# Transposes pinned directly ahead of the way up, statistics later in the tiles, and two reads moved, in a one-core transformer block

## The chip, the cores and the metric

The kernel runs on one core of a Trainium2 chip. A core has five engines, each with its own queue of instructions that it works off in order: PE (TensorE, matmuls and transposes; its weight loads, PEld, overlap with its matmuls), DVE (VectorE), ACT (ScalarE), POOL (GpSimd) and SP (SyncE, which here only issues DMAs). They meet at semaphores. Sixteen DMA engines move data between HBM and the core's memory. The metric is the device time of one execution in microseconds (us), here the median of several runs.

## What is computed

One block of a Perceiver-like transformer on x of 32 x 64 rows of 512 numbers, in fp32, cut to its core:

```python
x = x + xattn(layernorm(x), ctx, mask)          # softmax(x ctx^T / sqrt(512)) ctx, 256 context rows a batch
x = x + mla(layernorm(x), ...)                  # 16 heads, low-rank q (384) and kv (128), wo: 2048 -> 512
x = x + ffn(layernorm(x), ...)

def ffn(h):
    logits = h @ gate_w                                       # 8 experts
    scale = top_k(logits, 2).sum()
    shared = square(relu(h @ up_w)) @ down_w                  # 512 -> 2048 -> 512
    y = shared + (h @ expert_weight) * scale
    return layernorm(y) * ln_gamma + ln_beta
```

## The kernel before

**Stages.** The 2048 rows are 16 tiles of 128 rows (two batches). In the profiled execution the tile loop (lines 512 to 600) runs from 0 to about 240 us: cross attention, first residual, the latent q and kv. Then the attention itself (240 to 550), the way out (wo, L1073 to L1143, 551 to 765), the way up (up_w, from L1145, 773 to about 930) and the way down (down_w, 930 to 1097). PE works on fp32r, so an operand is split into a part h, rounded to fp32r (a copy by ACT, L147), and the rest l (a subtraction by DVE, L149), and a product is three matmuls: h h, h l, l h. The three large products also use a scheme with seven products of half blocks in place of eight; its sums ahead are POOL's, its sums behind are `combine` (one ACT copy L160, then DVE L162, L163, L165, L166, L168). The way out has 8 blocks of 256 rows by 8 values of k, 64 units u; the way up has 4 row blocks b by 8 units k, in the order `ORDER = (0, 1, 5, 6, 7, 2, 3, 4)`, of 42 matmuls each. A unit writes four PSUM banks, of which there are two sets; it can write a bank when the combine of the unit two before has read it.

**Order of work.** A framework's scheduler fixes the order on each engine's queue at compile time, by a model of its own, and sets the semaphores. `after(ins)` and the `pins` arguments say only that what follows is ordered behind `ins` in that order; they are no waits on the chip.

**The tile loop.** Iteration i scores tile i, reads out tile r = i - 1 (residual, normalisation with index b) and makes latents of tile q = i - 2. `stats(i + 1)` is the layer norm's statistics of the tile after the next: two DVE steps lnst_a, lnmv_a (L133, L135), DVE's rst_a (L123) and POOL's power rs_a (L127). For i of 4 to 14 it is written ahead of `a_q`; for i of 1 to 3 it stands behind `rooted["b.."]`, DVE's rst_b of tile r. `norm` then makes xn (DVE, L139) with rs_a; `a_x` does the same with rs_b. Both go through PE transposes (psy) and the split xh (ACT), xl (DVE L149). `psc` are PE's transposes of the next context.

**The way out.** For unit u, `left(u + 2)` splits the operand hl; `seven` does the matmuls (L723 with the high part first, L725 with the low). Weights for a unit are reads (`read_slot`) and splits (`put_slot`, two ACT casts wh and two DVE subtractions wl) into slots, the weights of wo first, those of the way up (`"up"`) in the last block's units: `UP_READ` and `UP_PUT` are the units of u % 8 of that block. After a block's last unit DVE adds the residual (`ox`, 512 KB, `o_load`, L948), normalises (`on`), PE transposes it (`ops`, L985), ACT and DVE split it (oh, ol), PE multiplies with the gate and the expert (`cpe`, `mm3` at L175), DVE takes the two largest (MAX8, gs), ACT scales (mo) and stores it (`mod<-mo`), and beta is added (`oo<-oo,beb`, L974). Beta is read once, broadcast to all partitions (256 KB), through POOL's queue at L922; the first residual at unit 10.

**The way up.** The split of its left operand is `right` (xr_0 and xr_2 by ACT, xr_1 and xr_3 by DVE). `settle(8, ...)` puts 8 PE transposes of a weight (their result is not used) ahead of the first products; with `None` as pin they are free to be placed by the scheduler:

```python
with after(settle(8, ps, wh[:, 0, 0], ident2, None) if b == 0 else None):
```

After each unit ACT squares the result (L1226, L1227), and in the first five units of b = 0 `put_slot(ORDER[n + 3], "up", pins=pins)` splits the weights of the unit three later.

Of the kernel before, what the change touches and what calls it, by code (L numbers as in the profile page):

```python
# [18 lines left out]
P = 128  # L19
B, S, D = 32, 64, 512  # L20
M = 256
NT = (B * S) // P
# [19 lines left out]
ORDER = (0, 1, 5, 6, 7, 2, 3, 4)  # L42
# [13 lines left out]
MULT_AT = (21, 25, 31, 39, 47, 55, 63)  # L56

FEATURES_AT = (2, 4)
UP_READ, UP_PUT = (1, 2, 5, 6, 7), (3, 5)

BETA_AT = 60

# [24 lines left out]
def perceiver_block(ctx: ExitStack, tc: tile.TileContext, x, mem, mask, wq_a, bq_a, qnw, wq_b, bq_b,  # L87
                    wkv_a, bkv_a, kvnw, wkv_b, wo, bo, gate, up, down, expert, gamma, beta, cs, out):
    nc = tc.nc
# [51 lines left out]
    def after(ins):  # L141
        return tc.issue_after(ins.ins) if ins is not None else ExitStack()
# [32 lines left out]
    def mm3(ps, pairs):  # L175

        n = len(pairs)
        for j, (ah, al, bh, bl) in enumerate(pairs):
            nc.tensor.matmul(ps, ah, bh, start=(j == 0), stop=False)  # L179
            nc.tensor.matmul(ps, al, bh, start=False, stop=False)  # L180
            nc.tensor.matmul(ps, ah, bl, start=False, stop=(j == n - 1))  # L181


    with ExitStack() as mla:
# [25 lines left out]
        with ExitStack() as pa:  # L210
# [145 lines left out]
            def stats(i):  # L356
                return ln_stats(sp, xts[i], 1e-5, f"a{i}")
# [157 lines left out]
            for i in range(NT + 2):  # L515
                q, r = i - 2, i - 1
                do_q, do_r = q >= 0, 0 <= r < NT
                if 1 <= i and i + 1 < NT:
                    if i > 1:
                        load_x(i + 1)  # L520
                    load(i + 1)
                if i == 1:
                    load_vectors()
                if i == 4:
                    load_turns()
                if do_q and i % 2 == 0:
                    hp[q // 2] = load_raw(q // 2)
                if i < NT:
                    with after(scored[0] if i == 1 else None):
                        cT = [a_t(i, 0), a_t(i, 1)]  # L530
                if 3 < i and i + 1 < NT:
                    mr = stats(i + 1)
                if do_q:
                    qk = ap.tile([P, 576], FP, tag="qk", bufs=1, name=f"qk{q}")
                    xh, xl, _ = xx.pop(q)
                    a_q(q, 0, qk, xh, xl)
                if do_r:
                    ex, rv = so.pop(r)
                    eT = a_e(r, ex)
                if i == 1:  # L540
                    prep_wa(1, raws[1])
                if do_q and i != NT:
                    a_q(q, 1, qk, xh, xl)
                    if i != 2:
                        lat = a_p(q, qk)
                if do_r:
                    x1 = a_r(r, eT, rv)
                if i == 2:
                    lat = a_p(q, qk, stats_of[f"b{r}"])
                if 1 <= i <= 3:  # L550
                    with after(rooted[f"b{r}"]):
                        mr = stats(i + 1)
                if i < NT:
                    xT = a_xT(i)
                if i == 1:
                    prep_wa(2, raws[2])
                if i == NT:
                    a_q(q, 1, qk, xh, xl)
                    lat = a_p(q, qk)
                if do_q and i % 2 == 1:  # L560
                    hp[q // 2] = fold_q(q // 2, *hp[q // 2])
                if q >= 2 and i % 2 == 0:
                    fold_o(q // 2 - 1, *hp.pop(q // 2 - 1))
                if do_q and i % 2 == 0:
                    hp[q // 2] += (load_rkv(q // 2),)
                if do_r:
                    xn = a_n(r, *x1)
                if do_q:
                    lat = a_z(q, *lat)
                if i < NT:  # L570
                    so[i] = a_s(i, cT, xT)
                if i == 1:
                    prep_wa(3, raws[3])
                    prep_wa(4, raws[4])
                if do_r:
                    xx[r] = a_x(r, xn)
                if do_q:
                    a_k(q, *lat)
                if i == 0:
                    last = prep_wa(0, raws[0])  # L580
                    load_small(masks[0])
                    with after(last[1]):
                        mr = stats(1)
                if i + 1 < NT:
                    norm(i + 1, mr)
                if i in (NT - 3, NT - 2):
                    load_q(i - NT + 3)
                if i in (NT - 2, NT - 1):
                    for k in range(NKQ):
                        split_q(i - NT + 2, k, xx[r][2])  # L590
# [3 lines left out]
        with ExitStack() as pb:  # L594
# [248 lines left out]
            n = len(units)  # L843
# [75 lines left out]
    sp = pc.enter_context(pool("o_small", 2))  # L919
    psb = ExitStack()  # L920
    beb = ap.tile([P, D], FP, name="beb")
    nc.gpsimd.dma_start(beb, beta.partition_broadcast(P))  # L922
    pss[1] = banks(psb.enter_context(pool("o_psb", space=PSUM)), "op1")
    oc = ExitStack()
    ocp = oc.enter_context(pool("o_c", 2))
# [7 lines left out]
    def o_load(blk):  # L933
        xt = ap.tile([P, 2, D], FP, tag="xt", name=f"ox{blk}")
        nc.sync.dma_start(xt, x1_d[blk].rearrange("t p d -> p t d"))
        return xt
# [65 lines left out]
    def o_expert(blk, xh, xl, _):  # L1002

        mo = mos.pop(blk, None) or ap.tile([P, 2, D], FP, tag="mo", name=f"mo{blk}")
        for tt in range(2):
            i = 2 * blk + tt
            sl = slice(tt * P, (tt + 1) * P)
            pes = []
            for c in (slice(256, NE), slice(0, 256)):
                pe = ps_t.tile([P, D], FP, tag="T", name=f"cpe{i}_{c.start}")  # L1010
                mm3(pe[:, 0 : c.stop - c.start], [
                    (xh[:, k, sl], xl[:, k, sl], wes[0][:, k, c], wes[1][:, k, c]) for k in range(NKD)
                ])
                pes.append(pe)
            t8 = sp.tile([P, 8], FP, tag="t8", name=f"t8{i}")
            nc.vector.max(t8, pes[0][:, 256:264])
            gs = sp.tile([P, 1], FP, tag="gs", name=f"gs{i}")
            nc.vector.tensor_tensor(gs, t8[:, 0:1], t8[:, 1:2], ALU.add)
            if tt:
                yield  # L1020
            nc.scalar.mul(mo[:, tt, 256:512], pes[0][:, 0:256], gs)
            nc.scalar.mul(mo[:, tt, 0:256], pes[1][:, 0:256], gs)
        nc.scalar.dma_start(mo_d[blk], mo)
        yield

    xr, xc, xw = {}, {}, []

    def read_x(b, kk, room=None, behind=None):

# [43 lines left out]
    for u, (blk, k) in enumerate(out_units):  # L1073
# [20 lines left out]
            read_slot(ORDER[i], "wo", i < 6, reads[-1])  # L1094
        if u in SLOT_AT:
            put_slot(ORDER[3 + SLOT_AT.index(u)], "wo", pins=low)
        if u == 10:
            xt[0] = o_load(0)
        if u == 30:
            with after(low[0]):  # L1100
                nc.scalar.copy(ident2, ident)
# [33 lines left out]
    xT = o_t(NB - 1, xns.pop(NB - 1), lambda: next(scaled))  # L1135
    for part in range(3):
        right(0, part, (dones[NB - 1][0], xT[2][1]))
    put_slot(ORDER[2], "up", pins=xT[2])
    for _ in o_expert(NB - 1, *xT):
        pass  # L1140
    pc.close()


# [2 lines left out]
    with ExitStack() as pu:  # L1146
# [3 lines left out]
        def up_seven(ps, k, b, n, steps):  # L1150
            wh, wl = (t[:, 0:7].rearrange("p a (k f) -> p a k f", k=2) for t in wts[k])

            def product(s, parts, first=False, last=False):
                i, j = SEVEN[s]
                for m, (kk, w, low) in enumerate(parts):
                    nc.tensor.matmul(  # L1156
                        ps[s // 2][:, s % 2], w[:, i, kk], xr[b, 2 * kk + low][:, j],
                        start=(first and m == 0), stop=(last and m == len(parts) - 1),
                    )

            most = [(0, wh, 0), (0, wl, 0), (0, wh, 1), (1, wh, 0), (1, wl, 0)]
            rest = [(1, wh, 1)]
            one, two = (0, 2, 4, 6), (1, 3, 5)
            late = None
            if n == 0:
                with after(settle(8, ps, wh[:, 0, 0], ident2, None) if b == 0 else None):
                    for s in one:
                        product(s, most, first=True)
            if n == 7:
                for s in one:  # L1170
                    product(s, rest, first=True)
                for s in (0, 2, 4):
                    product(s, most, last=True)
                for s in two:
                    product(s, rest, first=True)
                if b + 1 < NB // 2:
                    late = right(b + 1, 3)
            for s in range(7):
                if n == 0 and s in one:
                    product(s, rest, last=True)  # L1180
                elif n < 7:
                    product(s, most + rest, True, True)
                elif s in two or s == 6:
                    product(s, most, last=True)
                if s in (1, 3, 5, 6):
                    with after(late if s == 3 else None):
                        next(steps)
# [238 lines left out]
```

## Time and profile before

| | us |
|---|---|
| median of three runs | 1103.54 (1102.34 to 1108.92) |
| the profiled execution | 1098.9 |
| its span, first to last instruction | 1096.7 |
| PE busy | 1066.9 |
| DVE busy | 769.0 |
| ACT busy | 546.1 |
| POOL busy | 508.1 |

The clock granted to PE was full (1.00) in every stretch looked at. In the profile a line of a timeline gives start, busy time, engine, line and operation, output<-input, shape, and in square brackets the engine's idle time just before it and what ended that. A pair of tiles in the loop takes 27.4 us in steady state; a unit of the way up takes 4.95 us. A wait list counts only the waits of one engine, by who ended them.

### The profile page before, as it was taken

Reading aid. Unit: us, or ns where it says so; the run is one execution under the profiler, and the core shown is the slowest. Engines: PE = TensorE matmul, PEld = TensorE weight load, DVE = VectorE, ACT = ScalarE, POOL = GpSimd, SP = SyncE. Lnnn points to the kernel's source line nnn. Section 1 sums busy time; section 2 is a strip of 40 time slices with the busy share of each in tenths; the row PEclk is TensorE's granted clock in tenths of the full one; section 3 lists DMA queues with packets and bytes.
Section 4 is the critical chain, followed back from the end, with each engine's and each line's share of the span. In section 5 each row is a group of like instructions: output and inputs, shape, how many; then the busy total and the mean of one; then the engine's idle time right before and its main releaser. Section 6 shows DMA issues by size and latency. Waiting matters only on the chain.

```text
span 1096.7 us, 26072 instructions
## 1 busy us (share of the span) xinstructions
PE 1066.9 (97%) x10201; PEld 983.6 (90%) x10201; DVE 769.0 (70%) x1369; ACT 546.1 (50%) x1051; POOL 508.1 (46%) x691
## 2 busy tenths in 40 slices
PE   8999999999999999999998999999999999999996
PEld 6667777679999999999988999999999999999996
DVE  5666666657666666656787866667785658898786
ACT  4444444533433444434475544445676567755553
POOL 2333333326788778874570000003238970065671
PEclk9999999999999999999999999999999999999999
DMA  8867666343776778655487776779646689998672
GB/s 259 263 216 231 206 212 203 124 161 121 260 234 245 260 247 294 249 207 195 160 324 276 263 241 213 231 235 359 218 156 202 221 247 366 310 309 257 206 232 79
DMA packets 195386, 254.67 MB, mean 232 GB/s; under 512 B 18544, under 2 KB 140032, under 8 KB 195264
## 3 DMA queue, kind: packets, MB, share of 16 engines
q1 hardware_dynamic: 190704, 240.92, 67.0%
q10 hardware_dynamic: 3456, 8.39, 2.2%
q0 software_dynamic: 1104, 3.70, 0.9%
q8 instruction: 80, 1.31, 0.5%
q14 instruction: 42, 0.34, 0.1%
HBM read 146.67 MB, written 106.30 MB: 231 GB/s over the span
## 4 chain that ended last, share of the span: by engine, by line
PE 59%; DMA 10%; POOL 9%; DVE 8%; issue 7%; ACT 5%; SPq 1%; DVEq 0%; POOLq 0%; ACTq 0%
PE up L1156 9%; PE pss L773 5%; PE psq L179 4%; PE psq L180 4%; PE psq L181 4%; PE op L725 3%; PE op L726 3%; PE op L723 3%; PE psv L817 3%; DMA hd<-uo 2%; PE pse L179 2%; PE pse L181 2%; PE pse L180 2%; DMA x1d<-xt 2%; DMA vd<-vw 2%
## 5 line engine op out<-in xcount | busy, mean ns | idle before, releaser
L755 DVE SCALAR_TENSOR_TENSOR qe<-pse,bqp,cq 64x256 f32<-64x256 f32 x256 | 123.7, 483 | 76.5 <-PE pse L181 70.7
L1156 PE MATMUL up<-xr,wh_up 128*128 128x256 f32 x896 | 157.6, 280 | 0.6 <-DVE uo L168 0.6
L1156 PEld LDWEIGHTS up<-xr,wh_up 128*128 128x128 f32 x896 | 137.5, 189 | 1.0 <-issue 0.7
L725 PE MATMUL op<-wh_wo,hl 128*128 128x256 f32 x448 | 124.4, 279 | 3.7 <-DVE hl L149 3.7
L723 PE MATMUL op<-wh_wo,hl 128*128 128x256 f32 x448 | 124.0, 280 | 0.6 <-ACT hl L147 0.6
L725 PE MATMUL dp<-wh_down,hl 128*128 128x256 f32 x448 | 124.5, 278 | 0.0
L723 PE MATMUL dp<-wh_down,hl 128*128 128x256 f32 x448 | 124.4, 278 | 0.0
L726 PE MATMUL dp<-wl_down,hl 128*128 128x256 f32 x448 | 124.3, 277 | 0.0
L149 DVE TENSOR_TENSOR hl<-c,hl 128x896 fp32r<-128x896 f32 x84 | 94.3, 1126 | 42.3 <-ACT hl L147 42.0
L1156 PE MATMUL up<-xr,wl_up 128*128 128x256 f32 x448 | 123.7, 280 | 0.0
L726 PE MATMUL op<-wl_wo,hl 128*128 128x256 f32 x448 | 123.5, 277 | 0.0
L147 ACT CAST hl<-c 128x896 fp32r<-128x896 f32 x84 | 79.0, 942 | 77.7 <-PE op L726 38.0
L179 PE MATMUL psq<-qa_hi,qh 128*128 128x256 f32 x384 | 112.5, 293 | 0.0
L180 PE MATMUL psq<-qa_hi,ql 128*128 128x256 f32 x384 | 106.4, 277 | 0.0
L181 PE MATMUL psq<-qa_lo,qh 128*128 128x256 f32 x384 | 106.2, 276 | 0.0
L725 PEld LDWEIGHTS op<-wh_wo,hl 128*128 128x128 f32 x448 | 84.3, 188 | 4.8 <-DVE hl L149 4.7
L723 PEld LDWEIGHTS op<-wh_wo,hl 128*128 128x128 f32 x448 | 83.6, 188 | 1.5 <-ACT hl L147 0.8
L723 PEld LDWEIGHTS dp<-wh_down,hl 128*128 128x128 f32 x448 | 84.6, 189 | 0.0
L725 PEld LDWEIGHTS dp<-wh_down,hl 128*128 128x128 f32 x448 | 84.1, 188 | 0.4 <-DVE hl L149 0.4
L1156 PEld LDWEIGHTS up<-xr,wl_up 128*128 128x128 f32 x448 | 84.2, 188 | 0.0
L726 PEld LDWEIGHTS op<-wl_wo,hl 128*128 128x128 f32 x448 | 84.1, 188 | 0.0
L726 PEld LDWEIGHTS dp<-wl_down,hl 128*128 128x128 f32 x448 | 84.1, 188 | 0.0
(233 smaller groups left out, 3146.6 us busy)
## 6 DMA issues: line engine op xcount, KB each, us to landing
c<-vd SPq DMA_DIRECT2D x58, 448.0 KB, 4.2
cx<-in_ctx SPq DMA_DIRECT2D x32, 512.0 KB, 4.6
vd<-vw SPq DMA_DIRECT2D x29, 512.0 KB, 3.6
hd<-uo SPq DMA_DIRECT2D x107, 128.0 KB, 3.3
hd<-uw SPq DMA_DIRECT2D x21, 512.0 KB, 3.3
dcw<-hd SPq DMA_DIRECT2D x18, 448.0 KB, 5.6
vd<-v SPq DMA_DIRECT2D x30, 256.0 KB, 3.5
wd_wo<-pw_wo SPq DMA_DIRECT2D x8, 896.0 KB, 4.9
```

Source lines behind the costliest of these rows:

```text
L147: copy = nc.scalar.copy(hi, src)
L149: return copy, engine.tensor_tensor(lo, src, hi.bitcast(FP), ALU.subtract)
L179: nc.tensor.matmul(ps, ah, bh, start=(j == 0), stop=False)
L180: nc.tensor.matmul(ps, al, bh, start=False, stop=False)
L181: nc.tensor.matmul(ps, ah, bl, start=False, stop=(j == n - 1))
L723: first = nc.tensor.matmul(ps[s // 2][:, s % 2], h[:, a], wh[:, b], start=(k == 0 and s % 2 == 0), stop=False)
L725: nc.tensor.matmul(ps[s // 2][:, s % 2], l[:, a], wh[:, b], start=False, stop=False)
L726: ins = nc.tensor.matmul(ps[s // 2][:, s % 2], h[:, a], wl[:, b], start=False, stop=last)
L755: rope = nc.vector.scalar_tensor_tensor(qe[64 * a : 64 * a + 64, :], pe[r, :], bqp[r, p : p + 1], cq[r, a, :], ALU.add, ALU.mult,)
L773: nc.tensor.matmul(ps[64 * j : 64 * j + 64, pj, b, :], qs[2 * pj + j][a][:, sl], kT[:, a, kt], start=(a == 0), stop=(a == 1),)
L817: nc.tensor.matmul(o, kv[a, i, :], t[a, bp, :], start=True, stop=True)
L1156: nc.tensor.matmul(ps[s // 2][:, s % 2], w[:, i, kk], xr[b, 2 * kk + low][:, j], start=(first and m == 0), stop=(last and m == len(parts) ...
```

## The change

It has five parts.

1. `mm3` returns its last matmul and `o_expert` keeps it; before the way up there are 4 instead of 8 transposes, pinned behind the last `cpe` matmul.
2. `UP_PUT` loses its second unit; the split of slot `ORDER[1]` of the way up is called after the last `right` of the way out, pinned behind `xT[2]` (the last split of oh and ol).
3. `stats(i + 1)` stands behind rst_b in all iterations.
4. Beta's read goes from POOL's queue to SP's, behind the first residual.
5. The first residual's read goes from unit 10 to unit 12, pinned behind the reads issued so far.

```diff
-UP_READ, UP_PUT = (1, 2, 5, 6, 7), (3, 5)
+UP_READ, UP_PUT = (1, 2, 5, 6, 7), (3,)
...
-            nc.tensor.matmul(ps, ah, bl, start=False, stop=(j == n - 1))
+            ins = nc.tensor.matmul(ps, ah, bl, start=False, stop=(j == n - 1))
+        return ins
...
-                if 3 < i and i + 1 < NT:
-                    mr = stats(i + 1)
...
-                if 1 <= i <= 3:
+                if 1 <= i and i + 1 < NT:
                     with after(rooted[f"b{r}"]):
                         mr = stats(i + 1)
...
     beb = ap.tile([P, D], FP, name="beb")
-    nc.gpsimd.dma_start(beb, beta.partition_broadcast(P))
...
-                mm3(pe[:, 0 : c.stop - c.start], [
+                made.append(mm3(pe[:, 0 : c.stop - c.start], [
...
-        if u == 10:
-            xt[0] = o_load(0)
+        if u == 12:
+            with after(reads[-1]):
+                xt[0] = o_load(0)
+                nc.sync.dma_start(beb, beta.partition_broadcast(P))
...
     for part in range(3):
         right(0, part, (dones[NB - 1][0], xT[2][1]))
+    put_slot(ORDER[1], "up", pins=(low[0], xT[2][1]))
     put_slot(ORDER[2], "up", pins=xT[2])
     for _ in o_expert(NB - 1, *xT):
         pass
+    ends = made[-1]
...
-                with after(settle(8, ps, wh[:, 0, 0], ident2, None) if b == 0 else None):
+                with after(settle(4, ps, wh[:, 0, 0], ident2, ends) if b == 0 else None):
```

In the order of the changed program, ACT's half of slot `ORDER[1]` stays where it was and DVE's half stands behind the copies xr_1, ahead of the next slot's; the four transposes stand between the last `cpe` matmul and the first matmul of the way up; and in the first eight units of the way up ACT and DVE take units 2 and 3, 4 and 5, 6 and 7 in pairs, where they took one after the other.

## The prediction

> **What bounds the kernel now.** I read the page first, from its busy shares to the chain that ended last:
>
> ```profile
> PE 1066.9 (97%) x10201; PEld 983.6 (90%) x10201; DVE 769.0 (70%) x1369; ACT 546.1 (50%) x1051; POOL 508.1 (46%) x691
> PE 59%; DMA 10%; POOL 9%; DVE 8%; issue 7%; ACT 5%; SPq 1%; DVEq 0%; POOLq 0%; ACTq 0%
> ```
>
> TensorE (PE) is busy 1066.9 of 1096.7 us, so an edit off PE counts only where it opens or closes a gap in PE. Second, windows over the stages touched (columns: window; length; busy us of PE, PEld, DVE, ACT, POOL; granted clock; DMA share; GB/s):
>
> ```profile
> 155.00:182.00 27.00, 26.64 (x187) 19.36 (x188) 17.55 (x44) 12.89 (x34) 9.51 (x21) 1.00 0.64 205
> 580.00:600.00 20.00, 16.94 (x140) 16.34 (x140) 14.48 (x18) 11.44 (x15) 0.00 (x0) 1.00 0.75 256
> 773.00:816.00 43.00, 42.43 (x363) 42.25 (x362) 35.53 (x56) 31.41 (x54) 12.11 (x15) 1.00 0.46 147
> ```
>
> The tile loop loses 0.36 us in 27, the way out 3.06 in 20, the way up 0.57 in 43. Third, who ends PE's waits (total, times, longest):
>
> ```profile
> PE op L725 <- DVE hl L149: 3.7, 4, 2.0
> PE psq L292 <- DVE x L434: 3.2, 7, 1.9
> PE ops L985 <- DVE on L139: 1.0, 1, 1.0
> PE cpe L179 <- ACT oh L147: 0.9, 2, 0.5
> PE up L1156 <- DVE uo L168: 0.6, 1, 0.6
> ```
>
> These five are what the change can win: 9.4 us, of which it reaches about 6 (below).
>
> **Part 1, the statistics.** In tiles 4 to 14 the three steps lnst_a, lnmv_a, rst_a (0.69, 0.18, 0.15 us) move behind rst_b. In an even tile the order on DVE is now:
>
> ```profile
> 169.57 0.15 DVE L123 TENSOR_SCALAR rst_b<-lnmv_b 128x1 f32<-128x1 f32 x1
> 170.41 0.55 DVE L139 TENSOR_SCALAR xn<-x,lnmv_b,rs_b 128x512 f32<-128x512 f32 x1 [0.70 <-POOL rs_b L127]
> 170.88 0.54 DVE L139 TENSOR_SCALAR xn<-xt,lnmv_a,rs_a 128x512 f32<-128x512 f32 x1
> 172.33 0.69 DVE L149 TENSOR_TENSOR xl<-psy,xh 128x512 fp32r<-128x512 f32 x1
> ```
>
> Both normalisations run in one breath after one wait for POOL. In the new order, lnst_a fits into that 0.70 wait and costs nothing; without that cover it is 0.69 per tile. But lnmv_a and rst_a now stand behind xn(b), and the second xn waits for POOL's rs_a, which starts only then: 0.18 + 0.15 + 0.57 (POOL's step) + 0.1 of hand-overs, so 170.88 becomes about 171.9. Behind it in DVE's queue stand the score step, the maximum and xl; the PE transposes of the context that start at 173.07, when xl has ended (172.33 + 0.69), start 0.8 to 1.0 later. Tile 2 already has this order, and shows the price:
>
> ```profile
> 33.45 0.73 DVE L139 TENSOR_SCALAR xn<-xt,lnmv_a,rs_a 128x512 f32<-128x512 f32 x1 [0.60 <-POOL rs_a L127]
> 35.17 0.66 PE L373 MATMUL psc<-ident,cx 128*128 128x128 f32 x4 [0.56 <-DVE xl L149]
> ```
>
> Six even tiles (4 to 14) at 0.9 give +5.4; the ends are 0.56 (tile 2) and 1.02 (all of the delay), so 3.4 to 6.1. Odd tiles normalise one tile only; tile 3, which has the new order too, took 12.62 us against 12.73 to 12.83 of later odd tiles: -0.1 on six, -0.6. In tile 5 lnst_a waits 2.02 us for the load xt (landed 67.2) with everything behind it; that is the 1.88 us gap of PE at 71.95, and the tile takes 16.30 us instead of 14.63. Issued later, it finds xt landed: -1.7. Next late there is nothing that the trace shows. Sum +3.1 (+1.1 to +4.4).
>
> **Parts 2 and 3, beta and residual.** Beta (256 KB) leaves POOL's queue (issue 569.66, 0.58 us, which come free for the sums and stores of vd behind it; counted inside the bound below) and stands on SP behind the residual (512 KB), which moves from issue 578.07 to two units later. Around 577 to 586 the DMA engines are full (share 1.02 in 560 to 580, 397 GB/s), and the weight vd of the way out lands 586.6, releases wl_wo at 586.89, that hl at 588.90, that PE at 590.04 after 2.05 us. Some 768 KB fewer in that stretch are at most 768/415 = 1.9 us; I take 1.6 of the gap's 2.05; two smaller gaps before it (0.62 at 584.13, where hl waits for a read landed 583.1, and 0.39 at 585.25) I leave as they are. What is late next: the same 768 KB now stand on SP ahead of a c read; the residual's add (1.22 us) goes ahead of hl of unit 16, whose slack (from its end to PE's first low product) is 0.98, and beta's add (1.21) ahead of hl of unit 19, slack 0.05: up to 0.2 + 1.2. DVE idles 0.84 ahead of one hl there (612.28, for ACT), which swallows part; I put 0.6 back. Sum -1.0; from -2.5 (the gaps of 2.05 and of 0.48 at 615.74 closed) to +1.4 (both adds stall in full, nothing won).
>
> **Parts 4 and 5, the settling transposes and slot ORDER[1].** Taking wl of that slot (2.63 us at 755.37) out from ahead of combine(7) lets the last normalisation start earlier, but its first wait is then PE's cpe (MAX8 at 763.22): -0.83 of the 1.02 and 0.43 gaps (ops waiting for on, cpe for oh). Of the 8 transposes, before, 3 and 4 lie in these gaps (765.75, 767.01) and one on the path (773.04); after, four lie on it, 0.11 each: +0.33. So the way up starts at about 772.6 instead of 773.07. The granted clock in 760 to 775 is 1.00 with 1.45 us of idle, and in 580 to 600 with one gap of 2.05; so I price fewer transposes at nothing more.
>
> The Trainium skill speaks against that: "TensorE: Matmul & The Clock Gate", Part 4 (PE-mode transpose), says transposes do not count as busy for the clock gate, and its table ("Why this matters") has an idle window of about 3 us drop the clock to half. By the page the stretch from 763.65 to 767.4 (gap, transposes, gap) would have been one such window already; the trace shows no drop. By it, one slow window would add an estimated 1.7 us to the sum; I leave it out.
>
> On DVE wl of ORDER[1] (2.0) now stands ahead of wl of ORDER[2], the last MAX8/gs and xr_3. From 770.99 - 0.83: wl to 772.2, wl to 774.2, MAX8/gs to 774.6, xr_3 in two halves to 775.5 and 776.8, while PE wants them at 774.9 and 776.2 or so: +1.2 in unit 0. The last mo leaves ACT after gs: its store is issued about 776.5 instead of 774.17, and the first L162 of the way up, which waits for that buffer, goes from 780.10 to about 782.4.
>
> Worst, the scheduler has turned the queues: where ACT and DVE now take one unit after another,
>
> ```profile
> 785.37 2.09 DVE L149 TENSOR_TENSOR wl_up<-wl_up,wh_up 128x1024 fp32r<-128x1024 f32 x2 [0.89 <-ACT wh_up L147]
> 790.10 2.10 DVE L149 TENSOR_TENSOR wl_up<-wl_up,wh_up 128x1024 fp32r<-128x1024 f32 x2 [0.32 <-ACT wh_up L147]
> ```
>
> with a pitch of 4.73 against PE's 4.95 per unit, the changed program orders units in pairs: both L160, both L162, both combines, acts, wh, acts, wh, then wl twice. That is a loop through two engines per pair: 1.4 (two L162) + 1.6 (rest of one combine) + 1.7 (acts after L168) + 1.7 (wh) + 2.1 (acts) + 1.7 (wh) + 1.4 (the last wl) = 11.6 us, against 9.9 of PE. Three pairs lose 1.7 each, 5.1, of which the slack of the first (about 1.1: wl ends 787.4, PE needs it at 788.0, and the L163 slack) is free, plus the 2.3 of the late store: 6.3, and unit 0's 1.2 is mostly swallowed by the same wait, not added. Carried through rows with these durations, unit 8 starts about 820.4 instead of 813.39 (+7.0); against the same chain for the old order, +7.6. I take +6.5 for parts 4 and 5 together. Ends: 2.5 (the store lands in its old 780.1 and half the pair loss is hidden) and 7.6.
>
> **Sum.** 3.1 - 1.0 + 6.5 = +8.6. The profiled execution took 1098.9 us (span 1096.7 and 2.2 around it); it becomes 1107.5. The median of the runs, 1103.5, lies 4.6 higher; with the same addition, 1112.1: slower by 0.8%, inside the 1% (11 us) that a measurement of this kernel can tell from no change.
>
> **Rivals.**
> *Faster.* The DMA relief decides: tile 5's wait (-1.7), the gap at 590.04 (-2.05) and the transition (-0.83) all close, and POOL's rs_a comes before xn(b) has ended in even tiles, and the pairs stay within PE's slack. For it: the two largest waits in the list are just these. Against: tile 2's 0.56. It decides if even tiles lose under 0.3 (6 x 0.3 = 1.8): -4.6 + 1.8 - 0.6 = -3.4 at most, and so about 1100. 0.15.
> *The pairs are hidden*, since an engine's queue is eager where the data are there: U costs 1, tiles 3.1, way out -1.0: +3.1, 1106.6. Against: 4.73 against 4.95 leaves only 0.2 per unit. 0.20.
> *Everything in full.* Tiles 4.4, way out +1.4, way up 7.6: +13.4, 1117. It decides if the two adds stall hl. 0.20.
> *The change does less than it says*: ACT's half of ORDER[1] stays in its place, only DVE's moves, and seven of eight transposes were free. This is in the sum already; alone it leaves 1103.5.
>
> **Numbers.** Forecast (1109 to 1115) 0.45, rivals 0.15, 0.20, 0.20. Range 1102 to 1119: it leaves out most of the faster case (0.10) and the end of the full one (0.06). Faster by over 1% would need 11 us, more than the five waits hold: 0.04. Slower by over 1% (above 1114.6): the full case and a third of the forecast's, 0.35. Within: 0.61.
>
> **What would show it.** In the changed profile: DVE's xn of even tiles waiting 0.5 to 0.6 for POOL rs_a, and PE's psc for xl six times; no 1.88 at tile 5; PE's up waiting for wl and L163 by 0.5 to 2 us in units 3 to 8; the mo store near 776.5; the op wait at 590 under 1 us. I am wrong if psc shows no wait, or if the eight units stay at 4.95.

## The result and the profile after

The changed kernel takes 1112.65 us (median of 11 runs, 1108.59 to 1116.76), the kernel before 1102.34 us in the same series (11 runs): ratio 1.0084, 95% interval 1.0067 to 1.0102. It is slower: by 9.3 us if the ratio is taken, by 10.3 if the two medians are subtracted. The profiled execution took 1109.2 us, its span 1107.0 against 1096.7.

The page after, busy shares and the chain that ended last:

```profile
PE 1065.6 (96%) x10197; PEld 980.7 (89%) x10197; DVE 767.5 (69%) x1369; ACT 544.6 (49%) x1051; POOL 507.4 (46%) x690
PE 52%; issue 12%; POOL 12%; DVE 9%; DMA 9%; ACT 6%; SPq 1%; DVEq 0%; POOLq 0%; ACTq 0%
```

The engines do the same work; PE's share falls because the span is longer. The windows that answer to those of before (the last begins and ends 5 and 10 us later, with the stage):

```profile
155.00:182.00 27.00, 25.62 (x180) 18.38 (x179) 16.89 (x43) 12.15 (x33) 9.10 (x18) 1.00 0.64 211
580.00:600.00 20.00, 16.72 (x138) 15.94 (x138) 14.61 (x14) 11.47 (x14) 3.51 (x4) 1.00 0.73 262
778.00:826.00 48.00, 43.41 (x362) 42.37 (x361) 37.26 (x61) 29.75 (x52) 11.79 (x12) 1.00 0.42 133
```

The tile loop now idles 1.38 us in 27 (0.36 before), the way out 3.28 in 20 (3.06), the way up 4.59 in 48 (0.57 in 43). And who ends PE's waits:

```profile
PE op L724 <- DVE hl L149: 5.7, 6, 2.0
PE psc L374 <- DVE xl L149: 5.4, 7, 0.8
PE up L1158 <- DVE uo L162: 3.3, 1, 3.3
PE dp L722 <- DVE up L163: 1.9, 1, 1.9
PE psq L293 <- DVE x L435: 1.6, 7, 0.2
PE up L1158 <- DVE xr L1063: 1.3, 2, 0.9
```

psc waiting for xl is the loop's new wait (0.6 before), L162 and xr are the way up's, and the wait of 1.9 us at the entry of the way down is new against this profile of the kernel before (its second profile, below, has it too). The longest wait for hl in the way out is still 2.0.

Where the 10.3 us of the two spans lie, by the starts of PE's matmuls of each stage (first scores; last latent transposes; first and ninth unit of the way up; and so on), in us:

| profile | start | tile loop | attention | way out | units 0-7 | rest of way up | way down | span |
|---|---|---|---|---|---|---|---|---|
| before | 9.74 | 222.95 | 318.74 | 221.64 | 40.31 | 117.78 | 165.51 | 1096.68 |
| changed | 8.95 | 226.89 | 319.86 | 222.28 | 45.24 | 117.70 | 166.05 | 1106.95 |

The loop lost 3.9 and the first eight units of the way up 4.9. The rest, 1.4 us, is spread over stages that the change does not touch, or touches without a clear effect. One profile is one execution: the way out took 221.6 to 229.3 us in five profiles that have it in the same form (the two of the kernel before, e1, e5, e6), so its 0.6 us here says nothing.

### The profile page after: what moved, and what is told of

Its sections match the earlier page's. It is cut to its first block, busy times and chain, and to the rows that moved or that the text cites. A ratio compares the mean times of both kernels' runs of the same rounds, so it can differ in the third digit from the quotient of the medians.

```text
span 1107.0 us, 26074 instructions
## 1 busy us (share of the span) xinstructions
PE 1065.6 (96%) x10197; PEld 980.7 (89%) x10197; DVE 767.5 (69%) x1369; ACT 544.6 (49%) x1051; POOL 507.4 (46%) x690
## 3 DMA queue, kind: packets, MB, share of 16 engines
q8 instruction: 80, 1.31, 0.5%
## 4 chain that ended last, share of the span: by engine, by line
PE 52%; issue 12%; POOL 12%; DVE 9%; DMA 9%; ACT 6%; SPq 1%; DVEq 0%; POOLq 0%; ACTq 0%
PE pss L772 5%; PE up L1158 5%; PE psq L179 4%; PE psq L180 4%; PE psq L181 4%; PE op L724 3%; PE op L725 3%; PE op L722 3%; PE psv L816 3%; POOL uw L155 2%; POOL c L155 2%; PE pse L179 2%; PE pse L181 2%; PE pse L180 2%; POOL dcw L155 2%
## 5 line engine op out<-in xcount | busy, mean ns | idle before, releaser
L1158 PE MATMUL up<-xr,wh_up 128*128 128x256 f32 x896 | 155.0, 278 | 5.2 <-DVE uo L162 3.3
```

The costliest lines, as they stand in the source:

```text
L1158: nc.tensor.matmul(ps[s // 2][:, s % 2], w[:, i, kk], xr[b, 2 * kk + low][:, j], start=(first and m == 0), stop=(last and m == len(parts) ...
```

## The experiments

### Each part alone

Four kernels hold one part each: `stats(i + 1)` moved (e1), slot `ORDER[1]` moved (e2), the two reads moved (e3), 4 pinned transposes (e4). The edits are the lines of the diff above that belong to the part.

> The kernel before with the statistics alone moved. Theory: the loop loses what it lost in the changed kernel, whose tiles took 12.62 and 15.71 us in turn instead of 12.73 and 14.63: PE waits for xl in six even tiles (about 1.1 us each), tile 5's wait of 1.9 us is gone; +3.9 us at the end of the loop and at the end of the kernel, ratio about 1.0035. Rival: a later stage has waits that swallow it; the loop ends 3.9 us later but the way out starts less than 1 us later, ratio 1.000 to 1.001.

> The kernel before with the split of slot ORDER[1] alone moved. Theory: the pairs of units on ACT and DVE come from this edit alone; between the starts of unit 0 and unit 8 of the way up 45 us instead of 40.3, most of it one wait of PE of over 2 us in unit 7 for DVE's L162; the gap of PE ahead of the last transposes of the way out falls from 1.0 to about 0.3; ratio 1.003 to 1.006. Rival: the loss at unit 7 is paid back, since PE's step from matmul to matmul is then 113.3 ns instead of 117.8 for the rest of the way up (24 units of 42, 4.5 us at most); ratio 0.999 to 1.001.

> The kernel before with beta and the first residual alone moved. Forecast's step: the wait of 2.05 us at 590 shrinks by 1.6, 0.6 is paid back, ratio 0.999. Rival, as the changed kernel's trace has it: vd lands 7.3 us after its issue instead of 9.2, but its issue is 1.1 us later, so the wait at 590 stays near 2.0 and two waits of 0.7 to 0.9 for hl follow; ratio 1.000 to 1.001.

> The kernel before with the transposes alone changed (4 pinned behind the last cpe matmul instead of 8 free). Theory: 3 more transposes stand on the path, 0.11 us each, and nothing else: +0.3 us, ratio 1.000. Rival (clock gate): without transposes in the gaps the granted clock falls below 1.00 in the stretch around the start of the way up and its first units take over 1 us longer in all, ratio 1.001 or more.

| kernel | ratio to before | 95% interval | tile loop | units 0-7 |
|---|---|---|---|---|
| e1, statistics | 1.0046 | 1.0026 to 1.0067 | 226.92 | 39.08 |
| e2, slot | 1.0041 | 1.0021 to 1.0061 | 221.81 | 46.36 |
| e3, reads | 0.9979 | 0.9959 to 0.9999 | 222.28 | 39.82 |
| e4, transposes | 0.9983 | 0.9963 to 1.0004 | 222.21 | 41.86 |

Two parts make the loss, each with its own stage and neither with the other's: the statistics lengthen the loop, the slot the first units of the way up. The rivals of e1 and e2 fall; nothing later pays either back. The reads alone gain a little (their interval ends just below 1). The transposes show no price in the times. The granted clock in e4's windows from 755 to 785 is 1.00, so the clock rival falls there. The 41.86 us of e4 hold a wait of 1.79 us in unit 7, at 808.44, and 3.4 us at half clock behind it. The kernel before has a wait of 1.59 us at the same place in its second profile (e12), without the drop of the clock, so neither is put down to the transposes.

### What the statistics cost

e5 orders xn(b) of the even tiles behind rst_a; e6 moves the statistics in odd tiles alone:

```diff
+                    with after(rooted[f"a{i + 1}"] if i in (4, 6, 8, 10, 12, 14) else None):
+                        xn = a_n(r, *x1)
...
-                if 3 < i and i + 1 < NT:
+                if 3 < i and i % 2 == 0 and i + 1 < NT:
...
-                if 1 <= i <= 3:
+                if (1 <= i <= 3 or i % 2 == 1) and i + 1 < NT:
```

(The first hunk is e5's, on top of e1; the others are e6's, on the kernel before.)

> As e1 (statistics moved in all tiles), but in the six even tiles the normalisation xn(b) is ordered behind rst_a, so that POOL's rs_a runs beside xn(b). Theory (the price is the wait for POOL that starts only behind xn(b)): POOL's 0.57 us is hidden, the even tile takes about 15.2 instead of 15.7 us, the loop ends about 3 us earlier than in e1, ratio to the kernel before 1.001 to 1.003. Rival (the price is the three DVE steps wherever they stand behind rst_b, or the delay of xn(b)): the even tile stays at 15.6 to 15.8, ratio 1.004.

> The kernel before with the statistics moved in the odd tiles alone. Theory: tile 5's wait of 1.9 us goes, odd tiles take 12.62 instead of 12.73 to 12.83, even tiles stay at 14.63: 2.0 to 2.5 us less at the end of the loop, ratio about 0.998. Rival (the load of tile 5 only moves its wait to another step): ratio 1.000.

e5: ratio 1.0036 (1.0014 to 1.0059). e6: 1.0010 (0.9992 to 1.0028). From tile 4 on the tiles of these two profiles, even and odd, repeat to 0.03 us (a tile is taken from its first scores to those of the next), so here the trace tells more than the times. DVE in an even tile of the changed kernel:

```profile
170.83 0.15 DVE L123 TENSOR_SCALAR rst_b<-lnmv_b 128x1 f32<-128x1 f32 x1
170.90 0.68 DVE L133 BATCH_NORM_STATS2 lnst_a<-xt 128x6 f32<-128x512 f32 x1
171.68 0.55 DVE L139 TENSOR_SCALAR xn<-x,lnmv_b,rs_b 128x512 f32<-128x512 f32 x1
172.14 0.17 DVE L135 BATCH_NORM_AGGREGATE lnmv_a<-lnst_a 128x2 f32<-128x6 f32 x1
172.35 0.15 DVE L123 TENSOR_SCALAR rst_a<-lnmv_a 128x1 f32<-128x1 f32 x1
173.17 0.55 DVE L139 TENSOR_SCALAR xn<-xt,lnmv_a,rs_a 128x512 f32<-128x512 f32 x1 [0.67 <-POOL rs_a L127]
```

The same steps in e5:

```profile
170.40 0.15 DVE L123 TENSOR_SCALAR rst_b<-lnmv_b 128x1 f32<-128x1 f32 x1
170.47 0.68 DVE L133 BATCH_NORM_STATS2 lnst_a<-xt 128x6 f32<-128x512 f32 x1
171.19 0.18 DVE L135 BATCH_NORM_AGGREGATE lnmv_a<-lnst_a 128x2 f32<-128x6 f32 x1
171.40 0.15 DVE L123 TENSOR_SCALAR rst_a<-lnmv_a 128x1 f32<-128x1 f32 x1
171.47 0.54 DVE L139 TENSOR_SCALAR xn<-x,lnmv_b,rs_b 128x512 f32<-128x512 f32 x1
172.46 0.55 DVE L139 TENSOR_SCALAR xn<-xt,lnmv_a,rs_a 128x512 f32<-128x512 f32 x1 [0.44 <-POOL rs_a L127]
```

And PE behind it, first before, where the sixteen transposes run without a wait, then in the changed kernel:

```profile
172.06 2.28 PE L373 MATMUL psc<-ident,cx 128*128 128x128 f32 x16
```

```profile
175.16 0.65 PE L374 MATMUL psc<-ident,cx 128*128 128x128 f32 x4 [0.80 <-DVE xl L149]
175.98 0.66 PE L374 MATMUL psc<-ident,cx 128*128 128x128 f32 x4 [0.17 <-ACT kT L499]
```

From rst_b to the second xn it is 1.31 us before (169.57 to 170.88), 2.34 in the changed kernel, 2.06 in e5. The even tile takes 14.63, 15.71 and 15.44 us. The delay of that one step (1.03 and 0.75) is within 0.06 us of the loss of the tile (1.08 and 0.81). On the way to PE it changes a little: counted from rst_b, xl starts 0.83 us later in the changed kernel (3.59 against 2.76) and 0.54 in e5, and PE then waits 0.17 more for ACT's kT, which it did not before. So the mechanism holds, but e5 fell between its two expectations: running POOL's rs_a beside xn(b) gives back 0.27 us, not 0.5, as xn(b) is then itself later (1.07 behind rst_b instead of 0.84) and the second xn still waits 0.44 us for rs_a. What is left of the price, 0.75 of 1.03, is the three DVE steps and POOL's rs_a standing behind rst_b at all; no run took these two apart.

In e6 the tiles from 4 on are as expected (even 14.65, odd 12.62, tile 5 without its wait), but the whole is no faster; its expected ratio, 0.998, lies outside the interval. Part of the reason is in the last section of experiments: of the seven profiles with the old order of the loop only the first has that wait in full, and the mean is 0.7 us. With 0.9 for six odd tiles that leaves 1.6 us to win, a ratio of 0.9985, which still lies just outside. In e6's own profile tile 1 took 13.22 us (11.6 to 11.9 in all others), so its loop was no shorter, at 223.83. What took the rest in the runs stays open.

### What the slot costs

e7 puts DVE's half of the slot behind the last xr; in the program's order the units of the way up then alternate again:

```diff
-    put_slot(ORDER[1], "up", pins=(low[0], xT[2][1]))
...
-        right(0, 3)
+        x3 = right(0, 3)
+        put_slot(ORDER[1], "up", pins=(low[0], x3))
```

> As e2 (split of slot ORDER[1] behind the way out), but DVE's half stands behind the last xr instead of ahead of it; with that the program's ACT and DVE take the units of the way up one after another again. Theory (the pairs and the split ahead of gs and xr make the loss, not the move): no wait over 1 us between units 0 and 8, which take 40 to 41 us, as before; the gap ahead of the last transposes of the way out is about 0.3 instead of 1.0; ratio 0.998 to 1.000. Rival (DVE has too much to do in the way up once the split is inside it): units 0 to 8 take 43 us or more, ratio 1.002 to 1.004.

The ratio is 1.0016 (0.9998 to 1.0034): not told from 1, and above what was expected. But the stage is settled: units 0 to 7 take 39.72 us with the split of the slot inside them, and DVE's first steps of the combines (L162) follow each other at 4.73 us again:

```profile
783.34 3.16 DVE L149 TENSOR_TENSOR wl_up<-wl_up,wh_up 128x1024 fp32r<-128x1024 f32 x2
...
794.02 0.68 DVE L162 TENSOR_TENSOR uo<-up,up 128x512 f32<-128x512 f32 x1
...
798.75 0.68 DVE L162 TENSOR_TENSOR uo<-up,up 128x512 f32<-128x512 f32 x1
```

The gap ahead of the last transposes of the way out is 0.30 instead of 1.02. What this profile loses instead is a wait of 2.67 us at 759 for one of the last hl, which waits for its read, and the clock behind it (6.8 us at half clock; see below). DVE at the end of the pairs in the changed kernel shows how they hurt:

```profile
786.20 0.69 DVE L162 TENSOR_TENSOR uo<-up,up 128x512 f32<-128x512 f32 x1 [3.08 <-DMA mod<-mo]
...
814.51 2.10 DVE L149 TENSOR_TENSOR wl_up<-wl_up,wh_up 128x1024 fp32r<-128x1024 f32 x2 [1.28 <-ACT wh_up L147]
816.52 0.95 DVE L1063 TENSOR_TENSOR xr<-xp,xr 128x768 fp32r<-128x768 f32 x1
...
819.75 1.05 DVE L1063 TENSOR_TENSOR xr<-xp,xr 128x768 fp32r<-128x768 f32 x1 [1.14 <-ACT xr L1065]
...
822.39 1.27 DVE L162 TENSOR_TENSOR uo<-up,up 128x512 f32<-128x512 f32 x2
```

PE's one long wait of the stage, in unit 7, ends with it:

```profile
823.21 0.36 PE L1158 MATMUL up<-xr,wh_up 128*128 128x256 f32 x1 [3.28 <-DVE uo L162]
```

Both L162 of the last pair stand behind one wl pair, four xr steps and ACT's work for them (814.5 to 822.4). Before, L162 of unit 6 stood behind the wl pair and two of the xr steps, but ahead of the other two:

```profile
804.29 2.10 DVE L149 TENSOR_TENSOR wl_up<-wl_up,wh_up 128x1024 fp32r<-128x1024 f32 x2 [0.32 <-ACT wh_up L147]
...
808.63 0.69 DVE L162 TENSOR_TENSOR uo<-up,up 128x512 f32<-128x512 f32 x1
...
811.39 1.13 DVE L1065 TENSOR_TENSOR xr<-xp,xr 128x768 fp32r<-128x768 f32 x1 [0.35 <-PE up L1156]
...
814.12 0.68 DVE L162 TENSOR_TENSOR uo<-up,up 128x512 f32<-128x512 f32 x1
```

Counted from the start of the way up, the first L162 of the pairs start at 8.2, 19.3, 30.8 and 44.4 us: 11.05, 11.52 and then 13.62 us apart. The pairs before the last cost PE little: units 1 to 6 take 4.95 to 5.03 us each. In unit 0 PE waits 1.3 us for xr, which stand behind the extra wl.

### Leaving one part out, combining, and the same program again

e9 is the changed kernel without the statistics' move, e10 without the slot's, e11 without the reads'. e8 joins what looked good: statistics moved in odd tiles alone, reads, transposes. e12 is the kernel before, unchanged.

> The kernel before with statistics moved in odd tiles alone, the two reads moved and 4 pinned transposes; the slot left as it was. Theory: the parts add: -2.2 (odd tiles) -1.5 (reads; e3 gave -2.3 with an interval that reaches to 0) +0 (transposes): 1099 to 1100 us, ratio 0.995 to 0.998. Rival (waits for DMA in the way out take back what the loop wins): ratio 0.999 to 1.001.

> The changed kernel with the statistics where they were. Theory (the parts add): even tiles back at 14.63, the loop 3.9 us shorter, ratio to the kernel before 1.0035 to 1.005. Rival (the parts alone give less than the whole change, 0.46 + 0.41 - 0.21 - 0.17 = 0.49% against 0.84%, because they hinder each other behind the loop): ratio under 1.003.

> The changed kernel with the split of slot ORDER[1] where it was. Theory: units 0 to 8 of the way up back at 39 to 42 us instead of 45.2, ratio 1.003 to 1.005. Rival (the pairs hardly matter in the whole, since the way up's end is set by another engine): units 0 to 8 shorter, but the rest of the way up longer by as much; ratio over 1.007.

> The changed kernel with beta and the first residual where they were. Theory (the parts add): without the reads' gain of 0.2% the ratio is 1.010 to 1.011, and the wait of PE for hl near 590 is over 2 us. Rival (in the changed kernel the reads gain nothing, its wait there was still 1.99): ratio 1.008 to 1.009.

> The kernel before, once more, for a second profile of the same program. Theory (some waits of the first profile are that execution's, not the program's): ratio 0.999 to 1.001; the tiles at 14.63 and 12.73 to 12.83 again, but tile 5 anywhere from 14.7 to 16.3 by when its load lands, and PE's step in the way up at 113.3 ns in other units than before. Rival: tile 5 at 16.3 and 117.8 ns in units 0 to 6 and 15 to 31 again.

| kernel | ratio to before | 95% interval | tile loop | units 0-7 |
|---|---|---|---|---|
| e8, odd tiles, reads, transposes | 0.9989 | 0.9974 to 1.0004 | 222.09 | 39.59 |
| e9, all but statistics | 1.0022 | 1.0001 to 1.0042 | 222.40 | 45.00 |
| e10, all but slot | 1.0032 | 1.0016 to 1.0048 | 227.74 | 40.01 |
| e11, all but reads | 1.0078 | 1.0056 to 1.0100 | 227.21 | 44.75 |
| e12, before again | 1.0001 | 0.9983 to 1.0020 | 222.96 | 40.09 |

Taking either costly part away takes some 0.5 to 0.6% away, as each alone had brought 0.4 to 0.5%; within the intervals the parts add. e9's ratio lies in the range of its rival (under 1.003), and its interval reaches into both. e10 is as its theory had it. e11 speaks for its rival: in the changed kernel the reads gain nothing that can be seen, and the wait of over 2 us near 590 that its theory expected is not there (the longest for hl is 0.96). e8, the best combination tried, is not told from the kernel before; e3 alone stays just below 1.

e12 matters most for how to read a profile. PE in the stretch of the way out that I priced, and DVE's step in tile 5, in this second execution of the same program:

```profile
585.74 0.74 PE L723 MATMUL op<-wh_wo,hl 128*128 128x256 f32 x4 [1.27 <-ACT hl L147]
586.87 0.38 PE L725 MATMUL op<-wh_wo,hl 128*128 128x256 f32 x1 [0.39 <-DVE hl L149]
589.88 0.39 PE L725 MATMUL op<-wh_wo,hl 128*128 128x256 f32 x1 [0.34 <-DVE hl L149]
```

```profile
66.81 0.69 DVE L133 BATCH_NORM_STATS2 lnst_a<-xt 128x6 f32<-128x512 f32 x1 [0.17 <-DMA xt<-in_x]
```

The wait of 2.05 us at 590 is not there; others are. Tile 4, which ended with tile 5's wait in the first profile (16.30 us), takes 14.62. In the seven profiles with the old order of the loop it takes 14.62, 14.69, 14.92, 15.54, 15.61, 15.66 and 16.30. The later tiles repeat within 0.2 us; the first two differ by up to 2 us between profiles.

## Why the prediction was right, and where not

Forecast 1112.1, measured 1112.65; the sum of 8.6 us against 9.3. The direction and both large mechanisms were right, and the sizes of the terms less so than the sum: the loop cost 1.8 us more than forecast, the reads came out about 1 us worse and the slot 1 to 2 us better. That these nearly cancel is luck. The prediction also put its own 8.6 us inside what a measurement of this kernel cannot tell from no change (1%); the interval of the ratio is 0.17% to each side, and the loss is well outside it.

**The statistics** were forecast at +3.1 (1.1 to 4.4; the upper end leaves out the -0.6 of the odd tiles, with it the forecast's own terms give 3.8). Over the profiles the loop takes 222.3 us with the old order (mean of seven, 221.6 to 223.0) and 227.2 with the new (mean of four, 226.9 to 227.7): +4.9. The mechanism, the second xn behind POOL's rs_a and xl behind it, is the one shown. Two terms were mis-sized. "Six even tiles at 0.9" is 1.08 each, just beyond the end of its range (1.02): of the 1.03 us at DVE's xn 0.83 arrive at PE's psc, where PE waits 0.80 for xl, and the wait for ACT's kT adds 0.17. And the "-1.7" of tile 5 was the wait of one execution; by the seven profiles it is 0.7 on the mean. Six even tiles at 1.08, six odd ones at about -0.15 and -0.7 for the wait give +4.9.

**Beta and residual** were forecast at -1.0. The step "I take 1.6 of the gap's 2.05" rested on a wait that the same program does not have in its second profile. Alone the reads give -0.2% (-2.3 us, with an interval down to nearly nothing), in the changed kernel nothing. There the vd of the wait landed 7.4 us after its issue instead of 9.2, but the 9.2 was that execution's too: the other profiles with the reads in their old place have 7.7 to 8.6, those with the reads moved 7.4 to 8.3. And POOL issued it 1.15 us later against the start of the way out.

The other mis-sized term is "I put 0.6 back" for the two adds. In the changed kernel PE waits behind both:

```profile
602.48 1.22 DVE L946 TENSOR_TENSOR oo<-oo,ox 128x1024 f32<-128x1024 f32 x1
610.36 1.23 DVE L972 TENSOR_TENSOR oo<-oo,beb 128x1024 f32<-128x1024 f32 x1
```

```profile
604.75 0.38 PE L724 MATMUL op<-wh_wo,hl 128*128 128x256 f32 x1 [0.94 <-DVE hl L149]
612.65 0.38 PE L724 MATMUL op<-wh_wo,hl 128*128 128x256 f32 x1 [0.70 <-DVE hl L149]
```

All five profiles with the reads moved have this pair of waits, 1.3 to 1.9 us in all and 1.65 on the mean; none of the nine others has more than 0.6 there. Ahead of the adds, in the first 42 us of the way out, PE waits 1.5 us for hl on the mean with the reads moved (0.7 to 3.3) and 2.8 without (1.5 to 4.9). By these means the reads win about 1.3 and pay back 1.65, which fits that the changed kernel gains nothing from them, though the spread is as wide as the difference. Why e3 alone comes out just below 1 stays open.

**Transposes** were priced at +0.33 on the path, and that is what they cost: from the first cpe matmul behind the last ops to the first product of the way up PE takes 6.70 to 6.74 us in the six profiles with four pinned transposes and 6.37 to 6.41 in the eight with the free ones. e4's ratio (0.9983, up to 1.0004) cannot show so little. From ops to that first cpe it is 1.84 us in all fourteen: PE's waits for oh and ol are 0.97 us in the changed kernel and 0.43 before only because the free transposes had stood in the same idle time. The gap ahead of ops fell from 1.0 to 0.3 as forecast, but it is not the slot's alone: 0.29 to 0.62 in the five profiles with the slot moved, and 0.30 to 1.02 in the nine without (0.77 on the mean).

**The slot** was forecast, with the transition, at +6.5. Units 0 to 7 take 45.3 us in the four profiles with pairs (44.8 to 46.4) and 40.3 in ten without (39.1 to 42.5): +5.1, or some 4.4 to 4.7 with the shorter gap ahead of ops. The mechanism was right: the first pairs follow each other at 11.05 and 11.52 us, where the forecast's loop has 11.6. The step that fell is "Three pairs lose 1.7 each". Units 1 to 6 lost under 0.2 us in all. The late store did not take 5.9 us: issued 5.0 us behind the start of the way up, it landed 3.1 later, and the first L162 started at 8.2 instead of the forecast 9.8; and PE had more slack than the forecast's 1.1 us. The last pair alone lost 3.3, because xr stands inside it (13.62 us instead of 11.52), which the loop of 11.6 us had left out. So the forecast's sign, waits of 0.5 to 2 us in units 3 to 8, was one wait of 3.28 us.

**The rivals.** "The pairs are hidden" is refuted by e2 and e10. "Faster" needed even tiles to lose under 0.3. "Everything in full" had the right size for the statistics (4.4), and its two adds did stall hl (1.65 us against 1.4), but the gain ahead of them was not nothing, and its 7.6 us for the way up was too much.

**The clock.** The prediction priced each wait of PE at its own length. In the two profiles compared here that holds; in other executions a wait cost more, as the last section shows. The stretch from 763.65 to 767.4 that the prediction names, which kept the full clock, also holds two cpe matmuls (at 766.66), so it is no clean case of a stretch without matmuls.

## What to carry to other kernels

A step that only feeds a distant consumer still occupies its engine's queue: moved next to a hand-over to a second engine, it delays all that stands behind, and on a chain without slack nearly the whole delay becomes time (xn 1.03 us later, the tile 1.08 longer). Before an edit is priced, compare the order of the whole program on each engine: moving one split re-ordered ACT and DVE for the next eight units, and that order, not the split's work, was the price (e7 does the same work in the old order at 39.72 us). Take terms that repeat within a profile, tile by tile, at their word; a wait for a DMA that stands once in a profile may be that execution's own, and a second profile of the same program is the cheapest experiment there is. Small waits that return in every profile, like the two behind the adds, can outweigh the gain from such a one-off wait.

## What the hardware showed unexpectedly

**Half clock behind short waits.** The same wait of PE in unit 7 is followed by two different clocks. The changed kernel, windows over it (columns as above; the granted clock is third from the end):

```profile
818.00:822.00 4.00, 1.93 (x18) 1.73 (x16) 2.86 (x3) 3.19 (x6) 3.30 (x4) 1.00 0.35 98
822.00:826.00 4.00, 2.79 (x24) 2.82 (x25) 4.00 (x10) 1.05 (x2) 1.05 (x1) 1.00 0.53 169
826.00:830.00 4.00, 4.00 (x38) 4.00 (x37) 1.27 (x3) 3.86 (x9) 3.14 (x5) 1.00 0.62 195
```

and e9, with a wait of 3.15 us instead of 3.28:

```profile
818.00:822.00 4.00, 1.54 (x14) 1.34 (x12) 2.87 (x4) 2.68 (x5) 3.81 (x4) 1.00 0.34 98
822.00:826.00 4.00, 3.30 (x19) 3.33 (x20) 4.00 (x10) 1.56 (x3) 0.54 (x1) 0.69 0.64 206
826.00:830.00 4.00, 4.00 (x33) 4.00 (x33) 1.24 (x4) 2.97 (x7) 3.66 (x6) 0.88 0.52 157
```

In e9 PE is busy for 3.30 us and does 19 matmuls; at full clock 24 took 2.79. In all fourteen profiles, from 545 us on to PE's last matmul, PE waited 46 times for 1.0 to 3.6 us, and 15 of these waits were followed by 3.4 us (twice 6.8) at a granted clock of 0.5. Such a stretch cost an estimated 1.3 to 2.7 us, 1.7 on the mean (what the steps in it took above 113.3 ns); the prediction's estimate of 1.7 us for one slow window, which it left out of its sum, has the right size. The shortest such wait was 1.10 us (e4, at 585), the longest without it 3.28; a sixteenth stretch (e8, at 755) began behind two waits of 0.93 and 0.74 us. So a wait of PE of 1 us or more costs, on the mean, some 0.6 us more than its length (15/46 of 1.7), and its cost differs between executions of one program. The first profiles of the kernel before and of the changed kernel had none of it from 545 us until PE's last matmul. The times fit this: of 96 runs of the kernel before, the ten with a mean granted clock of 0.991 or 0.992 took 1106.3 us on the mean, the twenty with 0.997 or 0.998 took 1102.3.

The Trainium skill, "TensorE: Matmul & The Clock Gate", in "Why this matters", asks for no idle gaps of PE over about 3 us. The rule's direction holds here; its threshold does not, by the 1.10 us, and the 3.28 us that went free shows that length alone does not decide. What does was not tried.

**Two steps at one clock.** At a granted clock of 1.00 PE's step from matmul to matmul in the way up is either 113.3 or 117.8 ns for many units on end. The kernel before in its two profiles, the first line from the first, the second from e12:

```profile
773.00:806.00 33.00, 33.00 (x282) 33.00 (x281) 25.95 (x42) 24.13 (x42) 5.83 (x8) 1.00 0.49 159
```

```profile
773.00:806.00 33.00, 33.00 (x292) 33.00 (x292) 26.73 (x46) 23.54 (x41) 6.94 (x8) 1.00 0.52 164
```

PE is busy throughout in both, and does 282 or 292 matmuls. A unit takes 4.95 or 4.76 us by it; in e10 units 8 to 31 all ran at 117.8, in e12 nearly all at 113.3. That is up to 4.5 us for the same work (24 x 0.19), though not all of it reaches the end (118.72 us from unit 8 to the way down in e10, 117.02 in e12): where the last 24 units ran at 113.3 throughout or nearly so, PE then waits at the entry of the way down for DVE's last L163 (1.9 us in the changed kernel, 1.87 in e12), and where the last ones ran at 117.8 (the first profile of the kernel before, e1, e8, e10, e11) it does not. What sets the step was not tried; the traces show it changing at or near waits.
